# A fused Macaron block in three passes: where the mask and addition of finished tiles, the gate part's copies and a few single steps stand in the hand-written order

## The chip, the cores and the metric

The kernel runs on one core of one Trainium2 chip. TensorE (PE in the profile) does the matmuls, VectorE (DVE) and ScalarE (ACT) read its results and do the elementwise work, GpSimd (POOL) does elementwise work on data in SBUF, and SyncE (SP) issues most transfers. PE writes its products into PSUM banks; a product can start in a bank only when the engines that read the bank's former content are done. Everything is fp32. The metric is the device time in microseconds of one execution, as the median of several runs.

## The reference

The input is 4 x 1024 tokens with an embedding of 1024. The block adds half a clustered feed-forward, then attention, then the same feed-forward again, each on a layer norm of the running sum:

```python
x = x + 0.5 * ffn(layernorm(x))
x = x + attn(layernorm(x))
x = x + 0.5 * ffn(layernorm(x))

def ffn(x):                        # x: 4096 tokens x 1024
    dots = softmax(x @ centroids.T / 0.1)          # 64 clusters
    hits = dots > 0.01
    query_sel = any(hits, axis=1)                  # per token
    row_sel = any(hits, axis=0)[assignments]       # per output, over ALL tokens
    dense = x @ weight.T + bias
    return where(query_sel[:, None] & row_sel[None, :], dense, 0)

def attn(x):                       # 32 query heads, 8 shared key/value heads, D = 32
    q, k, v = x @ Wq + bq, x @ Wk + bk, x @ Wv + bv
    scores = einsum('bsdh,bseh->bsde', q, k) / sqrt(D)   # attention over D, within one token
    return einsum('bsde,bseh->bsdh', softmax(scores), v)
```

The row mask of the feed-forward needs the gates of all tokens. No tile can be finished before all gates are known.

## The kernel before

**Tiles and passes.** The tokens are cut into NT = 32 tiles of 128. Because of the row mask the kernel goes over the tiles three times. The first pass computes the gates and the dense output of the first feed-forward and stores the latter (`d1`) in HBM. The second pass (loop `for s in range(NT + 5)`, L898 to L1016) loads x and `d1`, masks and adds (`first_added`), normalizes, projects to q, k and v, does the attention, adds it (`second_added`), normalizes again and computes the gate part of the second feed-forward. The third pass (L1019 to L1093) computes the rest of the second feed-forward, masks it, adds it and writes the output. Tiles 26 to 31 are "kept" in SBUF from the second pass to the third; the others travel through HBM (`y2`, `xTd`, `d2`).

**Winograd products.** Large products are done for two tiles at once with seven half-size products in place of eight. In the feed-forward this is `winograd` (L258), a generator that yields after each product. Its order is: product 1 into a bank u, product 5 into v, product 2 into p, product 6 accumulated onto u, product 7 into y, product 3 into a further bank, product 4 accumulated onto y. After each product but the second, DVE adds what is ready into the rows of the output d (L270): one addition after products 1, 2, 7, 3 and 4, three after product 6. A product that accumulates onto u has to wait until the earlier addition has read u. Each product is four matmuls of 128x384 (L279); four PSUM banks serve them. The sums of the two tiles' halves that the products 5, 6, 7 and 3 take as input are `token_sums` (L252 to L255, four POOL instructions per pair), and the differences of weight blocks are `weight_sums` (L240). In the second pass `project_two` does the same for q, k and v of tiles 4 to 29 (`PAIRED`), in steps that are set between other PE work; its additions are L733 to L753.

**The gate part.** The columns of the feed-forward weight are cut into three parts; the first two go through the Winograd pairs and the third, with the 64 centroids behind it, is an ordinary product (`ffn_part`, L209). In the second pass `gate_2` issues it: ACT copies the dense part out of the bank (L221), DVE takes the maximum and difference of the gate's logits (L330, L332). `transposed` (L202, L203) turns a normalized tile with eight PE transposes into two banks, each copied out by ACT. `moments` (L159 to L162) computes the layer norm's statistics: bn_stats and bn_aggr on DVE, then a square root on ACT; `normed` (L168 to L177) makes the scales on DVE and normalizes on ACT. `first_added` is a mask on DVE (L388) and an addition on POOL (L399).

**The order is written by hand.** Each engine works through its instructions in the order in which the Python code emits them, and there is no scheduler. So a line that is moved in the code moves each instruction that it issues on that instruction's own engine, past the instructions of the lines it is moved over. Generators (`steps`, `two`, `held`, `normal`, `qsums`) let pieces of several computations be put between each other. The banks and the row buffers (26 of 512 KB, tag "row") are given out in turn.

**Third pass.** For each pair, the loads of the pair two ahead are issued on SP, then POOL makes the sums for the next pair (`ahead_3`), then the seven steps of `winograd` run. `added` (L1038 to L1041) finishes a tile: mask on DVE (L388), addition on DVE (L1040), and the output transfer on ACT's queue. The two `added` of a pair stand behind its last step, and the kept tiles' `added` stand behind the third and the sixth step of the first pairs.

**Drain and start of the second pass.** `held` are two Winograd pairs of the first pass, of which some steps are left to fill the first three rounds of the second. At the end of the second pass (s = NT + 2 and NT + 3) the first Winograd pair of the third pass, tiles 28 and 29, begins.

## Time and profile before

| | |
|---|---|
| median of 3 runs | 1350.83 us (1348.01 to 1351.83) |
| profiled execution | 1344.48 us |
| span of its trace | 1342.8 us, mean granted TensorE clock 0.998 |
| PE busy | 1313.6 us, 98% |
| DVE, POOL, ACT busy | 874.0, 581.8, 524.7 us |
| third pass, pairs | 19.14 us from one to the next (tiles 6 to 23) |
| second pass, two tiles | 34.95 to 36.28 us |

In a line of the timeline the first number is the start and the second the duration, both in us; then come engine, line of the kernel, operation and the tiles written and read. "x8" is the number of instructions put together in the line, and the brackets give the idle time ahead of it and what ended it. A PE line with x8 is four matmuls, each recorded as two. In the list of groups the numbers after the bar are the busy time in us and the mean of one in ns. A line of the windows begins with the window and gives for PE, PEld, DVE, ACT and POOL the busy us with the number of instructions, then the granted clock as a share of full speed, the share of the DMA engines that was busy, and GB/s.

### The profile page before, as it was taken

What the parts mean: (1) busy time and instruction counts of PE and PEld (TensorE: products, weight loads), DVE (VectorE), ACT (ScalarE), POOL (GpSimd) and SP (SyncE); (2) the same over time, 40 slices, a digit from 0 to 9 for tenths busy, and PEclk for the clock granted to TensorE, in tenths of its full rate; (3) what the DMA queues carried; (4) which work ended last, traced back from release to release, by engine and by line L of the source; (5) the groups of instructions that cost most, each with busy time, mean ns of one, the idle gap of its engine ahead of it and who ended that gap; (6) DMA issues with size and microseconds to landing.
All of it is one profiled execution on the core that took longest, in us unless ns stands there. A gap on an engine that the chain in (4) does not pass through costs nothing.

```text
span 1342.8 us, 22211 instructions
## 1 busy us (share of the span) xinstructions
PE 1313.6 (98%) x8486; PEld 823.7 (61%) x8486; DVE 874.0 (65%) x1709; ACT 524.7 (39%) x843; POOL 581.8 (43%) x443
## 2 busy tenths in 40 slices
PE   8999999999999999999999999999999999999998
PEld 7666666666665665666666666666666555555554
DVE  4565544554435368888888888878877358656655
ACT  4443434343411355666666666666633100000000
POOL 3511132232212255666666666666433316544540
PEclk9999999999999999999999999999999999999999
DMA  8477666668514255455656666665641257456421
GB/s 291 89 166 137 162 146 145 160 134 190 115 66 188 74 174 174 145 171 183 190 184 195 189 193 194 197 182 166 195 121 38 73 173 276 154 196 202 162 103 66
DMA packets 295770, 213.42 MB, mean 159 GB/s; under 512 B 240048, under 2 KB 254640, under 8 KB 295664
## 3 DMA queue, kind: packets, MB, share of 16 engines
q1 hardware_dynamic: 277712, 164.00, 44.9%
q0 software_dynamic: 8736, 30.68, 6.2%
q10 hardware_dynamic: 9216, 17.33, 3.4%
q8 instruction: 67, 1.10, 0.4%
q14 instruction: 39, 0.32, 0.1%
HBM read 127.77 MB, written 84.18 MB: 158 GB/s over the span
## 4 chain that ended last, share of the span: by engine, by line
PE 39%; DVE 8%; DMA 4%; issue 4%; POOL 2%; SPq 1%; ACT 1%; DVEq 0%; POOLq 0%; ACTq 0%
PE st L279 15%; PE qs L717 11%; PE ff L209 8%; DVE d L388 3%; DMA qkvd<-qkv 2%; PE tp L202 2%; DVE bn L159 2%; POOL x L864 2%; PE pq L209 2%; PE sc L793 1%; PE po L835 1%; DMA ot<-od 1%; DVE o L847 1%; SPq L767 1%; DMA qk<-qkvd 1%
## 5 line engine op out<-in xcount | busy, mean ns | idle before, releaser
L209 PE MATMUL ff<-wc,xT 128*128 128x320 f32 (+1 forms) x1088 | 307.6, 436 | 1.6 <-ACT wc L492 0.7
L209 PEld LDWEIGHTS ff<-wc,xT 128*128 128x128 f32 x1088 | 204.8, 190 | 92.5 <-ACT xT L203 1.0
L252 POOL TENSOR_TENSOR ts<-xT 128x512 f32<-128x512 f32 x31 | 42.4, 1367 | 296.0 <-PE st L279 187.9
L279 PE MATMUL st<-wc,xT 128*128 128x384 f32 x496 | 170.1, 486 | 0.0
L270 DVE TENSOR_TENSOR d<-st,d 128x384 f32<-128x384 f32 x157 | 86.4, 552 | 123.3 <-PE st L279 121.0
L773 POOL TENSOR_TENSOR kd<-qk,tmask 128x1024 f32<-128x1024 f32 x32 | 60.6, 1894 | 173.3 <-DMA qk<-qkvd 166.2
L279 PE MATMUL st<-wqkv,ts 128*128 128x384 f32 x360 | 123.7, 493 | 11.0 <-DVE d L270 11.0
L279 PEld LDWEIGHTS st<-wc,xT 128*128 128x128 f32 x496 | 94.0, 190 | 63.4 <-issue 0.2
L279 PE MATMUL st<-ws,ts 128*128 128x384 f32 x384 | 131.5, 486 | 0.0
L159 DVE BATCH_NORM_STATS2 bn<-x 128x6 f32<-128x512 f32 x132 | 84.5, 682 | 45.6 <-DMA x<-in_L_attn_x_dram 24.0
L388 DVE SCALAR_TENSOR_TENSOR d<-d,qsel,mask 128x1024 f32<-128x1024 f32 (+2 forms) x68 | 112.9, 1661 | 0.4 <-issue 0.2
L279 PEld LDWEIGHTS st<-wqkv,ts 128*128 128x128 f32 x360 | 68.2, 192 | 63.3 <-issue 19.6
L399 POOL TENSOR_TENSOR x<-x,d 128x1024 f32<-128x1024 f32 x32 | 75.4, 2357 | 71.2 <-DVE d L388 54.8
L717 PE MATMUL qs<-wc,ts_2q 128*128 128x384 f32 x312 | 106.2, 490 | 0.0
L279 PEld LDWEIGHTS st<-ws,ts 128*128 128x128 f32 x384 | 72.7, 190 | 49.4 <-issue 0.8
L162 ACT ACT_TABLE_LOAD x31 | 39.8, 1283 | 147.7 <-DVE mv L161 146.3
L270 DVE TENSOR_TENSOR d<-st,brow 128x384 f32<-128x384 f32 x93 | 51.2, 550 | 66.1 <-PE st L279 66.1
L203 ACT COPY xT<-tp 128x512 f32<-128x512 f32 x138 | 73.1, 581 | 32.6 <-PE tp L202 31.7
L279 PE MATMUL st<-wc,ts 128*128 128x384 f32 x248 | 85.2, 486 | 0.0
L202 PE MATMUL tp<-ident,xn 128*128 128x128 f32 x552 | 75.2, 276 | 8.5 <-ACT xT L203 6.5
L717 PEld LDWEIGHTS qs<-wc,ts_2q 128*128 128x128 f32 x312 | 58.2, 190 | 40.5 <-issue 2.6
L202 PEld LDWEIGHTS tp<-ident,xn 128*128 128x128 f32 x552 | 62.6, 141 | 28.4 <-ACT xT L203 9.3
(122 smaller groups left out, 2081.6 us busy)
## 6 DMA issues: line engine op xcount, KB each, us to landing
x<-in_L_attn_x_dram SPq DMA_DIRECT2D x64, 512.0 KB, 4.4
d<-d SPq DMA_DIRECT2D x64, 512.0 KB, 4.4
out_dram<-x ACTq DMA_DIRECT2D x30, 512.0 KB, 5.1
xb<-in_L_attn_x_dram SPq DMA_DIRECT2D x108, 128.0 KB, 4.6
y<-x POOLq DMA_DIRECT2D x26, 512.0 KB, 3.1
xTd<-xT POOLq DMA_DIRECT2D x26, 512.0 KB, 4.9
xT<-xTd SPq DMA_DIRECT2D x26, 512.0 KB, 4.8
x<-y SPq DMA_DIRECT2D x26, 512.0 KB, 4.8
```

Of the source, the lines that this page charges most:

```text
L159: nc.vector.bn_stats(st[:, i, :], src[:, i * 512 : (i + 1) * 512])
L162: nc.scalar.activation(mv[:, 1:2], mv[:, 1:2], AF.Sqrt, bias=eps)
L202: nc.tensor.transpose(tp[:, j, :], xn[:, k * P : (k + 1) * P], ident)
L203: nc.scalar.copy(t_[:, 4 * h : 4 * h + 4, :], tp)
L209: nc.tensor.matmul(p, src[:, k, :], wts[:, k, lo:hi], start=(k == 0), stop=(k == KT - 1))
L252: nc.gpsimd.tensor_tensor(s1, a21, a22, ALU.add)
L270: nc.vector.tensor_tensor(out, ps, other, ALU.add)
L279: nc.tensor.matmul(ps, src[:, k, :], wts[:, k, :], start=(k == 0 and onto is None), stop=(k == 3), skip_group_check=onto is not None,)
L388: nc.vector.scalar_tensor_tensor(d[:, sl], d[:, sl], qsel[which][:, t : t + 1], mask[:, sl], ALU.mult, ALU.mult)
L399: nc.gpsimd.tensor_tensor(xt[t], xt[t], dt_.pop(t), ALU.add)
L717: nc.tensor.matmul(ps, src[:, k, :], wts[:, k, :], start=(k == 0 and onto is None), stop=(k == 3), skip_group_check=onto is not None,)
L773: nc.gpsimd.tensor_tensor(kd, qk[:, :, D:].unsqueeze(2).to_broadcast([P, NBLK, 4, D]), tmask.unsqueeze(1).unsqueeze(3).to_broadcast([P, NB ...
```

## The change

Four places of the order are changed. The computation stays the same.

In the third pass the mask and addition of a finished pair's tiles stand no longer together behind the pair's last step. They are put off (`done`): one behind the first step and the other behind the third step of the next pair. The kept tiles' come behind the fifth and sixth step.

In the second pass, on odd steps, the gate part of one tile and the transposes of the other are emitted ahead of the statistics of a third. On PE nothing changes places. On ACT the copies L221 and twice L203 go ahead of the square root L162, and on DVE L330 and L332 go ahead of L159 and L161. On step 29, whose successor is not in `PAIRED`, the transposes are emitted by a later line, behind the normalization.

At the start of the second pass the left-over Winograd steps run as two, one and one in the first three rounds in place of one, one and two; two stores on SP go ahead of two loads. The third difference of weights is made a round earlier, and the fourth on POOL in place of DVE.

In the drain, the first three steps of the pair 28, 29 are emitted ahead of the statistics of tile 31.

```diff
-        qsums = weight_sums(wqkv, qts, [nc.gpsimd] * 3 + [nc.vector])
+        qsums = weight_sums(wqkv, qts, [nc.gpsimd] * 4)
...
-            if s == 4:
+            if 3 <= s <= 4:
                 next(qsums)
...
+            if paired and odd and s + 1 in PAIRED:
+                gate_2(a)
+                xT[f] = transposed(xn3.pop(f), f"3_{f}")
             if paired and (not odd or s + 1 not in PAIRED):
                 fo = attend(st, qkv.pop(b)[1], b)
-            if s == 4:
-                next(qsums)
+            if s == NT + 2:
+                dt_[a] = row(f"d3_{a}")
+                steps = winograd(s - 6, s - 5, ss, ts, None, 3)
+                for _ in range(3):
+                    next(steps)
             if has(g):
                 mv = moments(xt[g], f"3_{g}")
...
             if paired:
-                if odd:
-                    if s + 1 in PAIRED:
-                        gate_2(a)
-                    xT[f] = transposed(xn3.pop(f), f"3_{f}")
-                else:
+                if not odd:
                     next(two)
                 between()
...
-                    i = s - 6
-                    if k == 2:
-                        dt_[a] = row(f"d3_{a}")
-                        steps = winograd(i, i + 1, ss, ts, None, 3)
-                    for _ in range(6 - k):
+                    for _ in range(1 if k == 2 else 3):
                         next(steps)
...
-                for _ in range(1 + s // 3):
-                    next(held[s // 3])
-                i = {2: NT - 4, 3: NT - 2}.get(s)
+                for _ in range(2 if s == 1 else 1):
+                    next(held[s // 2])
+                i = {1: NT - 4, 3: NT - 2}.get(s)
                 for i in (i, i + 1) if i else ():
                     nc.sync.dma_start(out=d1[i], in_=dt_.pop(i))
...
+        done = iter(())
         for a in range(0, FIRST_KEPT, 2):
...
             for i in range(7):
                 next(steps)
-                if i in (2, 5):
-                    for t in kept:
-                        added(t)
-                        break
+                for t in done if i in (0, 2) else kept if i in (4, 5) else ():
+                    added(t)
+                    break
...
-            if not last:
-                added(a)
-                added(a + 1)
+            done = iter((a, a + 1))
```

## Prediction

> **What bounds the kernel now.** I read the page's busy times first, then what TensorE (PE) waited for, then the timelines around each of those waits. The page says that one engine fills the span:

> ```profile
> PE 1313.6 (98%) x8486; PEld 823.7 (61%) x8486; DVE 874.0 (65%) x1709; ACT 524.7 (39%) x843; POOL 581.8 (43%) x443
> ```

> The change adds and removes no matmul, so it can only win or lose the remaining 1342.8 - 1313.6 = 29.2 us in which PE stood idle, plus what a low clock adds. The waits of PE, as line waited for, us in total, times, longest:

> ```profile
> PE st L279 <- DVE d L270: 11.0, 10, 2.4
> PE tp L202 <- ACT xT L203: 6.5, 10, 1.1
> ...
> PE qs L717 <- DVE qkv L750: 0.8, 1, 0.8
> ...
> PE qs L717 <- DVE sc L190: 0.5, 1, 0.5
> PE ff L209 <- DVE d L270: 0.4, 1, 0.4
> ```

> Three stalls, then: Winograd products waiting for VectorE (DVE), transposes waiting for copies on ScalarE (ACT), and a few single ones. Everything off PE is hidden unless it feeds one of these.

> **Third pass.** PE and DVE around one pair of tiles:

> ```profile
> 1148.51 2.74 PE L279 MATMUL st<-wc,xT 128*128 128x384 f32 x8
> ...
> 1157.26 5.40 PE L279 MATMUL st<-wqkv,ts 128*128 128x384 f32 x16 [0.84 <-DVE d L270]
> ...
> 1167.65 2.74 PE L279 MATMUL st<-wc,xT 128*128 128x384 f32 x8
> ```

> ```profile
> 1148.71 0.56 DVE L270 TENSOR_TENSOR d<-st,d 128x384 f32<-128x384 f32 x1 [2.02 <-PE st L279]
> 1149.19 1.92 DVE L388 SCALAR_TENSOR_TENSOR d<-d,qsel,mask 128x1024 f32<-128x1024 f32 x1
> 1151.14 2.17 DVE L1040 TENSOR_TENSOR x<-x,d 128x1024 f32<-128x1024 f32 x1
> 1153.24 1.75 DVE L388 SCALAR_TENSOR_TENSOR d<-d,qsel,mask 128x1024 f32<-128x1024 f32 x1
> 1155.02 1.63 DVE L1040 TENSOR_TENSOR x<-x,d 128x1024 f32<-128x1024 f32 x1
> 1156.57 0.54 DVE L270 TENSOR_TENSOR d<-st,brow 128x384 f32<-128x384 f32 x1
> ```

> Products start 2.58 us apart (1148.51, 1151.09, 1153.67), so seven cost 18.06; the pair takes 1167.65 - 1148.51 = 19.14, 1.08 more. The fourth product accumulates onto the first one's bank (`onto=u`), so it must wait for the DVE addition that reads u. That addition is ready at 1151.25 and runs at 1156.57, behind the two `added` calls (7.4 us of L388 and L1040). Nine pairs (6 to 22) start 19.14 apart; pair 4, with two kept tiles' additions in its predecessor, takes 20.17. Lost: 9 x 1.08 + 2.11 = 11.8.

> After: let T count from the pair's first product. The u addition runs at 2.7 to 3.3. `added(a)` follows at 3.3 to 7.4 with the slow pair of durations above (4.1; without GpSimd (POOL) beside it L388 and L1040 take 1.27 and 1.22 at 1086 us, so 2.5). The third product's addition comes at 7.9 to 8.45, `added(a+1)` to 12.5 at worst, the three additions of the fourth product then end at 14.1, that of the fifth at 14.7. The last product, which accumulates onto the fifth's bank, starts at 15.48. Cover: 0.8 us with every L388 and L1040 slow, about 3 otherwise. I take the whole 11.8. The output transfers move with the additions, 3 to 6 us later on ACT's queue, which has no other work in this pass; SyncE's loads into the freed rows (1172.48 to 1181.39 here) then move too, and POOL's token sums with them. The token sums that start at 1165.32 feed a product that starts at 1167.65 + 19.14 + 2.58 = 1189.4; they last 6 us, so 6 us of lateness fits in a lead of 24.

> **Second pass, odd steps.** ACT runs the square root of `moments` ahead of the gate part's copies (L221, L203), and the square root waits for statistics:

> ```profile
> 890.50 0.29 ACT L162 ACTIVATE mv<-mv,eps 128x1 f32<-128x1 f32 x1 [2.04 <-DVE mv L161]
> 890.70 0.35 ACT L221 COPY d<-ff 128x256 f32<-128x256 f32 x1
> 890.95 1.07 ACT L203 COPY xT<-tp 128x512 f32<-128x512 f32 x2
> ```

> ```profile
> 891.59 0.65 PE L202 MATMUL tp<-ident,xn 128*128 128x128 f32 x4 [1.00 <-ACT xT L203]
> ```

> ff ended at 888.1 and ACT was free at 888.45, so the three copies run at 888.45 to 890.1 after the change and the transpose at 891.59 finds its bank. From one odd step's ff to the next the eleven full periods are 34.95 to 36.28 us; the shortest, 34.95, I take as the floor. The sum over it is 6.66, and 1.3 for the first step makes 8.0 (the recorded waits alone, 5.7). PE's own order stays. On DVE the gate's maximum and difference (L330, L332, 0.5 us) now precede bn_stats (1.29 + 0.21). Here they finish before x arrives from POOL at 888.93. In steps where x arrives first, bn and the mask behind it slip by up to 1.8 us (DVE's idle before this bn, 1.76) plus 1.5. What that delays is the mask, POOL's addition behind it and the next projection's additions (L739), which had 0.77 to 1.3 us to spare ahead of their PE reader. I take 6.5, with ends at 0 and 8. The square root itself, later by up to 1.4 us, is needed a step later.

> Step 29 loses: its transpose is not among the early ones and now stands behind square root, scales and the 1.25 us normalization of tile 26. The copies of tile 25 move from 962.81 to about 964.9, and the transpose and the product at 964.02 wait for them: -1.9, once.

> **Start of the second pass.** The fourth weight difference (L240) leaves DVE for POOL, the third moves one step up, the held products of the first pass move up and two stores of d pass two loads on SyncE. The 1.75 us of L240 on DVE at 518.35 stand ahead of bn_stats, the normalization, and the copies and additions that PE awaited at 524.15 (0.87) and 525.60 (0.79). The wait of 0.46 at 515.38 came from a mask on DVE that took 4.23 us at 509.94 while POOL ran L240 (3.44 us from 509.64); with POOL's row pushed 4.6 us on, that pair meets no more. Together 2.1, and the chain's remainder makes 2.3. [...] I take +2.3, ends -2 and +2.7.

> **Drain.**

> ```profile
> 1044.53 4.41 PE L279 MATMUL st<-wqkv,ts 128*128 128x384 f32 x8 [2.38 <-DVE d L270]
> ```

> ```profile
> 1041.61 1.29 DVE L159 BATCH_NORM_STATS2 bn<-x 128x6 f32<-128x512 f32 x2 [4.60 <-POOL x L864]
> ```

> ```profile
> 1044.00:1046.00 2.00, 1.47 (x3) 0.89 (x4) 0.94 (x2) 1.24 (x1) 0.00 (x0) 0.58 0.79 281
> ```

> The two additions PE needs queue behind statistics of tile 31, which wait for x (1041.61). After the change they run first, inside the 4.60 us idle. Saved: 2.38 of wait, 0.37 of the following ff wait. The product also took 4.41, where 2.74 is usual, at a granted clock of 0.58. [...] The row shows the drop directly behind this gap and nowhere else in the drain; the 1.88 us gap at 1136 brought none. I follow the row: ff starts at 1046.15, not 1050.18, gain 4.0, low end 2.4. Statistics of tile 31 slip by 0.5, covered until its transpose at 1062.

> **Sum.** 11.8 + 6.5 - 1.9 + 2.3 + 4.0 = 22.7, against the profiled execution's 1344.48: 1321.8. The median of three runs is 1350.83, 6.4 above that execution; the same share gives 1350.83 x (1 - 22.7/1344.48) = 1328.0.

> **Rivals.**
> - *The stall in the third pass only moves.* POOL's sums and L1035 now meet both separated `added`; if each takes 4.1 us and the u addition starts late, the last or sixth product waits and half of 11.8 stays: 1334. For: the alternating rows above. Against: the cover of 0.8 even then.
> - *The second pass gives nothing.* The later mask takes at L739 what the copies gave: 1328.0 + 6.5 = 1334.5. For: the small spare of 0.77. Against: in the step shown x arrives last.
> - *Slower.* The same mechanism outright: bn behind the gate slips by 1.8 + 1.5 = 3.3 in each of 12 pairs, less 1.3 spare, 2.0 x 12 = 24 lost and 6.5 not gained: 1358.5. It decides from (22.7 - 6.5)/12 = 1.35 us per pair. Against: DVE's idle of 1.76 before bn in the step shown ends on x, not on the gate.

> **How the numbers follow.** The forecast has 0.62, the first rival 0.13, the second 0.13, mixtures near no change 0.05, slower 0.07. A measurement of this kernel can tell about 0.3% (4 us) from no change. Faster 0.62 + 0.13 + 0.13 = 0.88, same 0.05, slower 0.07. Low end: 2 us of the pass-2 and start bounds and 4 of the runs' spread below 1328, 1321; high end: both rivals together, 1328 + 5.9 + 6.5 = 1340, plus 1: 1341. The forecast alone: 1323 to 1333.

> **What would show it.** Right: pairs 4 to 22 start 18.06 apart with no wait on L270; no PE wait on L203 from 530 to 930; the clock stays at 1.00 at 1044; one L203 wait near 964. Wrong: PE waits on L739 at the projection's fifth product, on POOL at 506, or on a DMA in the third pass.

## The result, and the profile after

The changed kernel takes 1326.70 us (median of 6 runs, 1325.35 to 1330.37) against 1349.96 us for the kernel before (6 runs, 1345.33 to 1352.20), a ratio of 0.9836 with a 95% interval of 0.9814 to 0.9859: 22 us, between 19 and 25. The profiled execution has a span of 1323.6 us in place of 1342.8. The waits of PE in it, in the columns of before:

```profile
PE tp L202 <- ACT xn L177: 2.2, 1, 2.2
PE tp L202 <- ACT xT L203: 1.9, 1, 1.9
...
PE sc L793 <- DMA qkvd<-qkv: 0.4, 1, 0.4
PE st L279 <- DVE d L270: 0.3, 1, 0.3
```

The 11.0 us behind L270 have become 0.3 (and those are in the first pass), and the ten waits on L203 are one. Two waits grew by some 0.4 us or are new: 2.2 us on L177 at the very start (1.8 before), in code that the change doesn't touch, and 0.4 us at the attention scores.

**Third pass.** PE around one pair, then DVE in the same stretch (L1038 is the addition of `added`, L1040 before):

```profile
1138.02 2.74 PE L279 MATMUL st<-wc,xT 128*128 128x384 f32 x8
...
1145.76 5.32 PE L279 MATMUL st<-wqkv,ts 128*128 128x384 f32 x16
...
1156.08 2.10 PE L279 MATMUL st<-wc,xT 128*128 128x384 f32 x6
```

```profile
1140.80 0.56 DVE L270 TENSOR_TENSOR d<-st,brow 128x384 f32<-128x384 f32 x1 [2.02 <-PE st L279]
1141.28 1.37 DVE L388 SCALAR_TENSOR_TENSOR d<-d,qsel,mask 128x1024 f32<-128x1024 f32 x1
1142.68 1.63 DVE L1038 TENSOR_TENSOR x<-x,d 128x1024 f32<-128x1024 f32 x1
1145.96 0.56 DVE L270 TENSOR_TENSOR d<-st,d 128x384 f32<-128x384 f32 x1 [1.65 <-PE st L279]
1146.43 1.28 DVE L388 SCALAR_TENSOR_TENSOR d<-d,qsel,mask 128x1024 f32<-128x1024 f32 x1
1147.74 1.22 DVE L1038 TENSOR_TENSOR x<-x,d 128x1024 f32<-128x1024 f32 x1
```

The pair takes 1156.08 - 1138.02 = 18.06 us, and the products run on without brackets. DVE adds u at 1140.80, as soon as it is there. The two `added` need 3.0 and 2.5 us where they took 4.1 and 3.4 before. In these rows they no longer run beside POOL's token sums; in pair 22 of the kernel before, where POOL was idle, each took 2.5 us as well, so the sums are the likely reason.

**Second pass.** ACT in an odd step:

```profile
882.57 0.35 ACT L221 COPY d<-ff 128x256 f32<-128x256 f32 x1
882.82 1.07 ACT L203 COPY xT<-tp 128x512 f32<-128x512 f32 x2
884.97 0.29 ACT L162 ACTIVATE mv<-mv,eps 128x1 f32<-128x1 f32 x1 [1.07 <-DVE mv L161]
```

The copies no longer wait for the square root. Every two tiles take 34.95 us, the floor, from 528.15 to 912.65.

**Step 29.** PE in the kernel before, then PE's one wait on L203 after the change, and the windows from there on:

```profile
963.09 1.09 PE L202 MATMUL tp<-ident,xn 128*128 128x128 f32 x8
964.02 10.49 PE L209 MATMUL pq<-wqkv,xT 128*128 128x384 f32 x32
```

```profile
957.73 1.11 PE L202 MATMUL tp<-ident,xn 128*128 128x128 f32 x4 [1.92 <-ACT xT L203]
958.64 11.75 PE L209 MATMUL pq<-wqkv,xT 128*128 128x384 f32 x32
```

```profile
958.00:960.00 2.00, 2.00 (x7) 1.38 (x7) 1.49 (x3) 1.97 (x5) 0.00 (x0) 0.50 0.98 292
960.00:962.00 2.00, 2.00 (x6) 1.12 (x5) 1.93 (x6) 0.66 (x3) 0.22 (x1) 0.70 0.81 148
```

A wait of 1.92 us, and behind it half the clock for some three microseconds: the projection took 11.75 us, 10.49 before.

**Drain.** PE at the first products of tiles 28 and 29:

```profile
1037.84 2.74 PE L279 MATMUL st<-wqkv,ts 128*128 128x384 f32 x8
1040.42 1.04 PE L202 MATMUL tp<-ident,xn 128*128 128x128 f32 x8
1041.92 1.34 PE L209 MATMUL ff<-wc,xT 128*128 128x320 f32 x4 [0.46 <-DVE d L270]
```

The fourth product takes 2.74 us, without a wait.

The two profiled executions can be set side by side stretch by stretch, each between the starts of the same PE instruction:

| stretch | before | after | difference | forecast |
|---|---|---|---|---|
| start to first full projection (same code in both) | 442.49 | 444.47 | +1.98 | 0 |
| to the first gate product (start of second pass) | 85.79 | 83.68 | -2.11 | -2.3 |
| to the gate product of step 29 | 429.40 | 421.60 | -7.80 | -6.5 |
| to the next gate product (step 29's loss) | 18.69 | 22.50 | +3.81 | +1.9 |
| to the first product of tiles 28, 29 | 57.88 | 57.85 | -0.03 | 0 |
| to the gate product behind the fourth product (drain) | 15.93 | 11.82 | -4.11 | -4.0 |
| to the first product of tile 4 | 78.16 | 78.04 | -0.12 | |
| to the first product of tile 24 (third pass) | 191.37 | 180.60 | -10.77 | -11.8 |
| to the end | 23.09 | 23.04 | -0.05 | 0 |
| sum | 1342.8 | 1323.6 | -19.2 | -22.7 |

This is one execution of each. The second row can come out smaller with the same code, as the second pass's block alone shows below.

### The profile page after: what moved, and what is told of

Read it like the earlier page. It is cut to its first block, busy times and chain, and to the rows that moved or that the text cites. A ratio compares the mean times of both kernels' runs of the same rounds, so it can differ in the third digit from the quotient of the medians.

```text
span 1323.6 us, 22208 instructions
## 1 busy us (share of the span) xinstructions
PE 1310.4 (99%) x8486; PEld 826.0 (62%) x8486; DVE 858.6 (65%) x1708; ACT 524.9 (40%) x843; POOL 575.4 (43%) x444
## 4 chain that ended last, share of the span: by engine, by line
PE 91%; DVE 4%; DMA 2%; ACT 2%; issue 1%; ACTq 0%; DVEq 0%; SPq 0%
PE st L279 39%; PE ff L209 21%; PE qs L717 17%; PE tp L202 4%; PE pq L209 4%; PE sc L793 2%; PE po L835 2%; DMA x<-in_L_attn_x_dram 1%; DVE bn L159 1%; DMA scd<-sc 1%; DVE d L270 0%; PE tpw L487 0%; ACT xT L203 0%; DVE d L388 0%; PE pm L382 0%
## 5 line engine op out<-in xcount | busy, mean ns | idle before, releaser
L209 PE MATMUL ff<-wc,xT 128*128 128x320 f32 (+1 forms) x1088 | 307.5, 436 | 1.5 <-ACT xT L203 0.6
L209 PEld LDWEIGHTS ff<-wc,xT 128*128 128x128 f32 x1088 | 204.7, 190 | 92.4 <-issue 1.0
L279 PE MATMUL st<-wc,xT 128*128 128x384 f32 x496 | 170.2, 486 | 0.0
L270 DVE TENSOR_TENSOR d<-st,d 128x384 f32<-128x384 f32 x157 | 86.0, 550 | 122.3 <-PE st L279 121.1
L279 PEld LDWEIGHTS st<-wc,xT 128*128 128x128 f32 x496 | 94.0, 190 | 63.6 <-issue 0.4
L279 PE MATMUL st<-ws,ts 128*128 128x384 f32 x384 | 131.6, 487 | 0.3 <-DVE d L270 0.3
L279 PE MATMUL st<-wqkv,ts 128*128 128x384 f32 x360 | 121.3, 486 | 0.0
L388 DVE SCALAR_TENSOR_TENSOR d<-d,qsel,mask 128x1024 f32<-128x1024 f32 (+2 forms) x68 | 106.3, 1563 | 0.1
L717 PE MATMUL qs<-wc,ts_2q 128*128 128x384 f32 x312 | 106.2, 490 | 0.0
L159 DVE BATCH_NORM_STATS2 bn<-x 128x6 f32<-128x512 f32 x132 | 84.3, 680 | 31.2 <-DMA x<-in_L_attn_x_dram 28.5
L279 PEld LDWEIGHTS st<-ws,ts 128*128 128x128 f32 x384 | 72.6, 190 | 50.2 <-issue 2.1
L279 PEld LDWEIGHTS st<-wqkv,ts 128*128 128x128 f32 x360 | 68.3, 190 | 48.1 <-issue 0.8
L203 ACT COPY xT<-tp 128x512 f32<-128x512 f32 x138 | 73.2, 581 | 30.4 <-PE tp L202 29.5
L279 PE MATMUL st<-wc,ts 128*128 128x384 f32 x248 | 85.1, 486 | 0.0
L270 DVE TENSOR_TENSOR d<-st,brow 128x384 f32<-128x384 f32 x93 | 51.2, 550 | 52.1 <-PE st L279 52.0
L717 PEld LDWEIGHTS qs<-wc,ts_2q 128*128 128x128 f32 x312 | 58.2, 190 | 40.5 <-issue 2.6
L202 PE MATMUL tp<-ident,xn 128*128 128x128 f32 x552 | 74.3, 278 | 4.2 <-ACT xn L177 2.2
L864 POOL TENSOR_TENSOR x<-x,ot 128x1024 f32<-128x1024 f32 x32 | 77.1, 2408 | 2.5
```

Source lines behind the costliest of these rows:

```text
L159: nc.vector.bn_stats(st[:, i, :], src[:, i * 512 : (i + 1) * 512])
L202: nc.tensor.transpose(tp[:, j, :], xn[:, k * P : (k + 1) * P], ident)
L203: nc.scalar.copy(t_[:, 4 * h : 4 * h + 4, :], tp)
L209: nc.tensor.matmul(p, src[:, k, :], wts[:, k, lo:hi], start=(k == 0), stop=(k == KT - 1))
L270: nc.vector.tensor_tensor(out, ps, other, ALU.add)
L279: nc.tensor.matmul(ps, src[:, k, :], wts[:, k, :], start=(k == 0 and onto is None), stop=(k == 3), skip_group_check=onto is not None,)
```

## The experiments

**Each part alone.** The four parts of the change were put singly into the kernel before: the third pass's loop, the second pass's block, the start (differences of weights and held products), and the drain. Six of the runs below were executed once each: the start alone, the drain alone, the differences undone, both additions together, the statistics first and the gaps. The 22 executions of the kernel before beside the first two of these spread from 1341.3 to 1350.7 us, so what is said of these six is read from their traces and not from their times. The third pass alone:

```diff
+        done = iter(())
         for a in range(0, FIRST_KEPT, 2):
...
-                if i in (2, 5):
-                    for t in kept:
-                        added(t)
-                        break
+                for t in done if i in (0, 2) else kept if i in (4, 5) else ():
+                    added(t)
+                    break
...
-            if not last:
-                added(a)
-                added(a + 1)
+            done = iter((a, a + 1))
```

> The kernel before with the third pass's edit alone. Theory: every pair from 4 on starts 18.06 us after the one ahead, with no wait on L270; from tile 4's first product to tile 24's first product 180.6 us in place of 191.4, so about 10.8 us off the time of before, ratio 0.992. Rival (the stall only moves to another product): 185 to 186 us and a new wait on L270 at the sixth or seventh product. The gap of 2.4 us in the drain is still there; if every gap of that length brings a low clock, its product takes 4.4 us again, and if it depends on where the gap falls, it may take 2.74.

Measured: a ratio of 0.9929 to the kernel before (0.9901 to 0.9957). From tile 4's to tile 24's first product 180.59 us, in a pair:

```profile
1131.55 2.74 PE L279 MATMUL st<-wc,xT 128*128 128x384 f32 x8
...
1139.29 5.32 PE L279 MATMUL st<-wqkv,ts 128*128 128x384 f32 x16
...
1149.61 0.81 PE L279 MATMUL st<-wc,xT 128*128 128x384 f32 x2
```

1149.61 - 1131.55 = 18.06, with no bracket on the fourth product. The third pass's part gives its 10.8 us by itself, and the stall did not move to another product. The gap in the drain was 2.71 us here, and its product took 2.82: no low clock (granted 1.00 from 1049 to 1053 us) behind a longer gap than that of before.

The second pass's block alone:

```diff
+            if paired and odd and s + 1 in PAIRED:
+                gate_2(a)
+                xT[f] = transposed(xn3.pop(f), f"3_{f}")
             if paired and (not odd or s + 1 not in PAIRED):
                 fo = attend(st, qkv.pop(b)[1], b)
...
-                if odd:
-                    if s + 1 in PAIRED:
-                        gate_2(a)
-                    xT[f] = transposed(xn3.pop(f), f"3_{f}")
-                else:
+                if not odd:
                     next(two)
```

> The kernel before with the second pass's edit alone (gate part and transposes ahead of the statistics, step 29 as in the change). Theory: two tiles take 34.95 us in all steps between the first and the last gate product, 7 us less in sum than before, and step 29 loses 1.9 us, or up to 3.8 if its gap brings a low clock; together 3 to 5 us off, ratio 0.996 to 0.998. Rival (DVE's later statistics and masks take it back): a wait on L739 at the projection and no gain.

Measured: ratio 0.9963 (0.9951 to 0.9975). No wait on L203 between the first step and step 29, where it was 1.95 us; this time the clock stayed at 1.00 behind it. From the first gate product to the projection of tile 30 it took 429.95 us in place of 435.74, 5.8 less. The projection did not wait on L739 anywhere.

The stretch ahead of it, from the first full projection to the first gate product, took 84.37 us in place of 85.79, though up to that product this run's order is that of the kernel before: the block acts first in the step of this gate product. The waits of 0.46 and 0.87 were not there, because a mask happened to start ahead of POOL's weight difference; the run with the differences undone comes back to it.

The start alone:

```diff
-        qsums = weight_sums(wqkv, qts, [nc.gpsimd] * 3 + [nc.vector])
+        qsums = weight_sums(wqkv, qts, [nc.gpsimd] * 4)
...
-            if s == 4:
+            if 3 <= s <= 4:
                 next(qsums)
...
-            if s == 4:
-                next(qsums)
...
-                for _ in range(1 + s // 3):
-                    next(held[s // 3])
-                i = {2: NT - 4, 3: NT - 2}.get(s)
+                for _ in range(2 if s == 1 else 1):
+                    next(held[s // 2])
+                i = {1: NT - 4, 3: NT - 2}.get(s)
```

> The kernel before with the edit at the start of the second pass alone (held products a round earlier, weight differences all on POOL and one a round earlier). Theory: from the first full projection's start to the first gate product 83.7 us in place of 85.8, the waits of 0.46, 0.87 and 0.79 gone, nothing else changed. [...]

Measured: 84.09 us, 1.7 less than before and 0.4 short of the theory. Of the four profiles with the order of before in this stretch, three have 85.71 to 87.56 (the last with a low clock) and one 84.37, so the gain differs from one execution to the next. The waits of 0.46, 0.87 and 0.79 are gone, but a new one of 0.79 stands at the attention scores:

```profile
504.94 1.06 PE L793 MATMUL sc<-kd,qk 32*32 32x128 f32 x64 [0.79 <-DMA qkvd<-qkv]
```

The line names a transfer, the store of the next tile's q, k and v, which is no input of these scores; POOL had made their keys a step earlier (490.82 in the profile of the change). But the scores are written where the last attention product lay (both are tiles of the one buffer "att"), and DVE still reads that in L847. DVE in this run shows why it is late:

```profile
498.93 3.02 DVE L388 SCALAR_TENSOR_TENSOR d<-d,qsel,mask 128x1024 f32<-128x1024 f32 x1
...
503.17 1.52 DVE L847 SCALAR_TENSOR_TENSOR o<-po,tmask,o 128x256 f32<-128x256 f32 x3
```

The mask takes 3.02 us where 1.27 is usual, beside POOL's third difference (L240, here 3.46 us from 497.40). Eight profiles have the difference at this place. In them the mask took 2.60 to 3.27 us and PE waited 0.37 to 1.05, in each 2.22 or 2.23 less than the mask took; in three profiles without it the mask took 1.27 or 1.28 and PE did not wait. So the wait is the mask's. And in all eight the mask ended 1.09 to 1.10 us behind the end of POOL's L240. In this run 1.93 us of L240 were left when the mask came, and the mask took 1.75 us longer than the usual 1.27: it lost about what was left of that instruction, and not its whole length of 3.46.

The drain alone:

```diff
+            if s == NT + 2:
+                dt_[a] = row(f"d3_{a}")
+                steps = winograd(s - 6, s - 5, ss, ts, None, 3)
+                for _ in range(3):
+                    next(steps)
             if has(g):
                 mv = moments(xt[g], f"3_{g}")
...
-                    i = s - 6
-                    if k == 2:
-                        dt_[a] = row(f"d3_{a}")
-                        steps = winograd(i, i + 1, ss, ts, None, 3)
-                    for _ in range(6 - k):
+                    for _ in range(1 if k == 2 else 3):
                         next(steps)
```

> The kernel before with the edit in the drain alone. Theory: the wait of 2.4 us on L270 in the drain is gone and the fourth product takes 2.74 us, so from the first product of tiles 28 and 29 to the gate product behind the transposes 11.8 us in place of 15.9. Rival (the low clock comes from elsewhere): the product takes 4.4 us still, 13.5 us.

Measured: 11.81 us, and no wait at the fourth product. The low clock went with the gap, as the theory had it: the product takes 2.74 us, 4.41 before. This profile has a low clock at another place, though, behind two short waits of 0.88 and 0.79 us at the start of the second pass; the kernel before has nearly the same two waits (0.87 and 0.79) and full speed behind them, a granted clock of 1.00 and 2.85 us for the product that takes 4.54 here:

```profile
528.39 4.54 PE L717 MATMUL qs<-wc,xT 128*128 128x384 f32 x8 [0.79 <-DVE qkv L750]
```

**The start with the differences undone.** In the changed kernel:

```diff
-        qsums = weight_sums(wqkv, qts, [nc.gpsimd] * 4)
+        qsums = weight_sums(wqkv, qts, [nc.gpsimd] * 3 + [nc.vector])
...
-            if 3 <= s <= 4:
+            if s == 4:
                 next(qsums)
...
+            if s == 4:
+                next(qsums)
             if s == NT + 2:
```

> The changed kernel with the third and fourth weight difference where they were before (third on POOL and fourth on DVE, both in round 4). Theory: the 1.75 us on DVE bring back the waits of 0.87 and 0.79 and the collision the one of 0.46, and from the first full projection to the first gate product it takes 85.3 to 85.8 us in place of 83.7. Rival (the held products' places did it): 83.7 to 84.

Measured: 85.22 us. The waits of 0.82 and 0.78 are back; the one of 0.46 is not, and that at the scores is gone. So the places of the differences are worth 0.9 to 1.5 us here (the eight profiles with the change's places have 83.68 to 84.35); of the 1.60 that the two waits cost, the wait at the scores takes the rest back, wholly or in part. The 0.46 is another matter. DVE's mask and POOL's L240 around it, in the kernel before and then in the second pass's block alone, whose order in this stretch is the same:

```profile
509.94 4.23 DVE L388 SCALAR_TENSOR_TENSOR d<-d,qsel,mask 128x1024 f32<-128x1024 f32 x1
509.64 3.44 POOL L240 TENSOR_TENSOR wc<-wqkv 128x1536 f32<-128x1536 f32 x1
```

```profile
513.10 1.19 DVE L388 SCALAR_TENSOR_TENSOR d<-d,qsel,mask 128x1024 f32<-128x1024 f32 x1
513.69 3.90 POOL L240 TENSOR_TENSOR wc<-wqkv 128x1536 f32<-128x1536 f32 x1
```

Before, L240 came 0.30 us ahead of the mask and the mask took 4.23 us; in the second run it came 0.59 us behind, and the mask took 1.19. PE's wait of 0.46 was gone, and that of 0.87 with it, as DVE came to the work behind the mask earlier. With the differences undone L240 starts two microseconds behind the mask (513.62 and 511.44; the mask takes 2.33), and there is no wait of 0.46 either. So the 0.46 hangs on which of the two starts first, by some tenths of a microsecond, and with the order of before it can fall either way. What the held products' places add to that is not shown.

**Step 29 mended.** The transposes ahead of that step's statistics:

```diff
+            if paired and odd and s + 1 not in PAIRED:
+                xT[f] = transposed(xn3.pop(f), f"3_{f}")
             if has(g):
                 mv = moments(xt[g], f"3_{g}")
```

Beside it ran the changed kernel once more, and the same with eight transposes of the identity, whose result nothing reads, in the idle time at the start:

```diff
         columns(7)
+        for i in range(8):
+            nc.tensor.transpose(bank(f"fill{i}")[:, :P], ident, ident)
         xT[0] = transposed(xn.pop(0), "1_0")
```

> The changed kernel once more, on the chip of the next three. Every theory: a ratio of 0.984 to the kernel before, within 0.003. The waits of 1.9 us at step 29 and of about 2 us at the start are there again; whether a low clock follows them may differ from the first profile.

> The changed kernel with the transposes of step 29 emitted ahead of that step's statistics. Theory: the wait of 1.9 us on L203 there is gone, and with it the low clock that followed in the first profile; from the gate product of step 29 to the projection of tile 30 6.3 us in place of 8.9, in all 2 to 4 us below the changed kernel, ratio 0.981 to 0.983. Rival (the banks are held by something else, DVE's gate or the attention): the wait stays at over 1 us.

> The last one with eight more transposes of the identity in PE's idle time ahead of the first token tile's transposes. Theory: these fill most of the 2.2 us gap there, so that the transposes behind it always take 1.1 and not 2.0 us; 0 to 1.5 us below the last one. Rival: PE runs them at half speed past the point at which the normalized tile is there, and loses about 0.3 us.

Measured, on one chip against the same runs of the kernel before: the changed kernel 0.9852 (0.9826 to 0.9877), 1324.94 us; with step 29 mended 0.9842 (0.9821 to 0.9864), 1323.67 us; with the eight transposes too 0.9820 (0.9799 to 0.9841), 1320.67 us. The second ratio is above the 0.981 to 0.983 expected, though its interval reaches down to them, and the last kernel is 3.0 us below the one ahead of it, more than the 1.5 expected. The intervals of the three overlap, though each of the four executions of the last (1320.50 to 1321.55) is quicker than each of the five ahead of it (1322.43 to 1324.83). What happened where is in the traces. ACT and PE at step 29, mended:

```profile
952.52 1.05 ACT L203 COPY xT<-tp 128x512 f32<-128x512 f32 x2
955.08 0.30 ACT L162 ACTIVATE mv<-mv,eps 128x1 f32<-128x1 f32 x1 [1.50 <-DVE mv L161]
955.90 1.24 ACT L177 ACTIVATE xn<-x,sc 128x1024 f32<-128x1024 f32 x1 [0.53 <-DVE sc L170]
```

```profile
955.17 1.09 PE L202 MATMUL tp<-ident,xn 128*128 128x128 f32 x8
956.10 4.36 PE L209 MATMUL pq<-wqkv,xT 128*128 128x384 f32 x13
```

The copies run two microseconds ahead of the square root and the transpose has no bracket: 956.10 - 949.77 = 6.33 us from the gate product to the projection, as expected, 8.89 in the change. From the first gate product to the first product of the drain it is 498.78 us against 501.95 for the change, 3.2 less, although the next gate product now waits 0.62 us for DVE. At the start, PE with the eight transposes:

```profile
8.49 0.71 PE L496 MATMUL fill<-ident 128*128 128x128 f32 x4 [1.10 <-DVE wc L490]
9.08 1.06 PE L202 MATMUL tp<-ident,xn 128*128 128x128 f32 x8
```

The largest gap there is 1.10 us in place of 2.25, and the token transposes take 1.06 us, 1.97 in the profile of the change. They are not late. This is one profile; that they will always do so isn't shown.

**Both additions together, behind the first step.**

```diff
-                for t in done if i in (0, 2) else kept if i in (4, 5) else ():
+                for t in done if i == 0 else ():
+                    added(t)
+                for t in kept if i in (4, 5) else ():
                     added(t)
                     break
```

> The changed kernel with both additions of the finished pair behind the first step of the next pair, not one there and one behind the third. Theory: what matters is that the first product's addition comes ahead of them; they end at 10.7 us at worst and the fourth product's additions are ready at 10.48, so pairs still start 18.06 us apart without a wait. Rival (it is the single placing that counts): a wait on L270 of 0.5 us or more at the sixth or seventh product in each pair, 18.6 us or more.

Measured: 18.06 us a pair and no wait on L270 in the third pass. DVE:

```profile
1143.30 0.56 DVE L270 TENSOR_TENSOR d<-st,brow 128x384 f32<-128x384 f32 x1 [2.02 <-PE st L279]
1143.78 1.28 DVE L388 SCALAR_TENSOR_TENSOR d<-d,qsel,mask 128x1024 f32<-128x1024 f32 x1
1145.09 1.63 DVE L1038 TENSOR_TENSOR x<-x,d 128x1024 f32<-128x1024 f32 x1
1146.64 1.27 DVE L388 SCALAR_TENSOR_TENSOR d<-d,qsel,mask 128x1024 f32<-128x1024 f32 x1
1147.95 1.23 DVE L1038 TENSOR_TENSOR x<-x,d 128x1024 f32<-128x1024 f32 x1
1149.09 0.55 DVE L270 TENSOR_TENSOR d<-st,d 128x384 f32<-128x384 f32 x1
```

That they are put singly is not what gives the gain in this pass. It is enough that u's addition comes first.

**Statistics first on DVE.** In the changed kernel bn_stats and bn_aggr go back ahead of the gate; the square root stays behind the copies:

```diff
             if paired and odd and s + 1 in PAIRED:
+                mv = moments(xt[g], f"3_{g}", False)
                 gate_2(a)
                 xT[f] = transposed(xn3.pop(f), f"3_{f}")
...
-            if has(g):
+            if paired and odd and s + 1 in PAIRED:
+                nc.scalar.activation(mv[:, 1:2], mv[:, 1:2], AF.Sqrt, bias=eps)
+            elif has(g):
                 mv = moments(xt[g], f"3_{g}")
```

(With `False`, `moments` leaves out the square root.)

> The changed kernel with bn_stats and bn_aggr put back ahead of the gate part on DVE; only the square root on ACT stays behind the copies. Theory: what PE waited for was ACT's order, so the second pass keeps its period of 34.95 us per two tiles and shows no wait on L203 before step 29. Rival (the gate's maximum and difference hold the bank): waits of 0.3 to 1 us at the transposes in the steps where x comes late, up to 7 us in sum.

Measured: no wait of the transposes on the copies ahead of step 29 (there 1.78 us), and a single one of 0.66 at a gate product, on the gate's difference (L333 here). So ACT's order is what had to change; DVE's order is worth about 1 us in the whole pass (from the first gate product to that of step 29 422.65 us, against 421.38 to 421.60 in the eight other profiles with the second pass's block; it was 429.40 before).

**Gaps of two sizes.** What happens to the clock when PE idles for two or three microseconds? In the third pass of the changed kernel:

```diff
             for i in range(7):
+                if i == 0:
+                    for t in done:
+                        added(t)
+                    for j in range(1 if a % 4 else 2) if 4 < a < 22 else ():
+                        idle = small.tile([P, 1], F32, tag="gmx", name=f"idle{j}_{a}")
+                        nc.vector.tensor_reduce(idle, mask, AX.X, ALU.max)
                 next(steps)
-                for t in done if i in (0, 2) else kept if i in (4, 5) else ():
+                for t in kept if i in (4, 5) else ():
                     added(t)
                     break
```

(The additions stand ahead of the pair's first step again, and the maxima behind them, which nothing reads, put u's addition off further.)

> The changed kernel with both additions ahead of the first product's addition, as before the change, and behind them on DVE one or two maxima of 1.2 us that nothing reads, in pairs 6 to 20 (one in pairs 6, 10, 14 and 18, two in 8, 12, 16 and 20). PE then idles about 2 and 3.2 us ahead of the fourth product at eight places. If the low clock depends on where a gap falls and not on its length alone, some of the products behind the 2 us gaps take 4.4 us and some 2.74, and those behind 3.2 us more often 4.4; a pair with the low clock costs about 1.8 us more. [...]

Measured, PE at gaps of both sizes:

```profile
1154.41 5.40 PE L279 MATMUL st<-wqkv,ts 128*128 128x384 f32 x16 [1.97 <-DVE d L270]
1175.80 5.40 PE L279 MATMUL st<-wqkv,ts 128*128 128x384 f32 x16 [3.09 <-DVE d L270]
...
1217.47 7.09 PE L279 MATMUL st<-wqkv,ts 128*128 128x384 f32 x16 [3.10 <-DVE d L270]
...
1260.83 5.40 PE L279 MATMUL st<-wqkv,ts 128*128 128x384 f32 x16 [3.10 <-DVE d L270]
...
1302.49 7.09 PE L279 MATMUL st<-wqkv,ts 128*128 128x384 f32 x16 [3.10 <-DVE d L270]
```

Four equal gaps of 3.1 us: two are followed by a product pair of 7.09 us, with a granted clock of 0.50 in 1219.47 to 1221.47 and 1304.49 to 1306.49, and two by 5.40 at 1.00. So at this length the gap alone does not settle the clock. The low clock expected behind some of the four of 1.97 did not come. A low clock costs 1.7 us here.

## Why the prediction was right, point by point

The forecast was 1328.0 us with a range of 1321 to 1341; the median is 1326.7. The span fell by 19.2 us and the sum named 22.7. Each term can be read from the table. The mechanisms named for the large terms are the ones that the runs show. That the sum came within 1.3 us of the median owes something to luck: 1.0 too much in the third pass and 1.3 too little in the second cancel, and step 29 and the start of the program went the other way by 3.9 in the profile.

- *Third pass, 11.8: the mechanism is right, the size is 1.0 too large.* The step that failed is "Nine pairs (6 to 22) start 19.14 apart", and the table of the profile before has it too ("tiles 6 to 23"). The ninth stall, that of tile 22, does not exist: from 1301.65 to 1319.71 it is 18.06, where POOL has no more sums to make and DVE is through in time. 8 x 1.08 + 2.11 = 10.75, and 10.77 was measured. The list of waits would have told: ten waits in all, one of them the drain's and one pair 4's, leave eight. The rival in which the stall only moves is excluded by the third pass alone and by the run with both additions together.
- *Second pass, 6.5: right, 1.3 too small.* The 1.5 us that I held back for DVE were not needed; nothing waited on L739, and the rival that ends slower did not begin to show. The floor, 34.95 in each step, was reached: 7.8 of the 8.0 named as the upper end.
- *Step 29, -1.9: the wait is right to the tenth (1.92), the price is not.* It was 3.81 in the profile, the other half of it from the low clock behind the wait. The step that failed is that the wait was costed at its length alone, while in the drain I had let the clock follow a gap of 2.38. What was allowed for one gap of some two microseconds had to be allowed for the other, as a chance: behind the same wait the second pass alone (1.95) kept the full clock.
- *Start, 2.3: 2.11, with its terms shifted.* The three waits went in these two profiles. Two of them were also missing in one of four profiles with the order of before, so the gain is 2.11 against this execution and would be 0.7 at most against that one (84.37 us, against 83.68 to 84.35 with the change's order). PE did not wait on POOL at 506. The slow mask beside a weight difference on POOL came at another place, 2.60 to 3.27 us where 1.27 is usual, and made PE wait at the scores, by way of a bank, for 0.37 to 1.05 us. For the low end of -2 that the prediction gives this term no run shows a source: the start alone gained 1.7 us with a wait of 0.79 at the scores in it.
- *Drain, 4.0: 4.11.* I took the row, with the low clock (0.58) directly behind the gap of 2.38 us, and the drain alone shows it right: the low clock went with the gap, and the product takes 2.74 us. Yet in the run of the third pass alone a gap of 2.71 us at the same place had none (granted 1.00), and there removing it would have been worth 14.67 - 11.82 = 2.9. The value taken was right for the profile, not for every run.
- *The unchanged start, 0: +1.98.* In this profile PE idled 2.25 us ahead of the first tile's transposes and ran them at half clock (granted 0.50 from 9.11 to 11.11; 1.97 us for 1.09), which made 1.4 of it. That part of the program is the same in both. It is one reason why the spans differ by only 19.2 and the medians by 23.3. The other is that the profiled execution of before, 1344.48, was quicker than each of the six timed runs of its kernel (1345.33 and more), while that of the change, 1325.35, is as quick as the quickest of its own. What made the slower executions of before slower is not shown; no trace of them was kept.
- *The range.* Its low end is named as 2 and 4 us below 1328.0, which is 1322 and not 1321. Nothing hangs on it.

## What to carry to other kernels

When an accumulating product must wait for a reader of its bank, ask what stands ahead of that reader on its engine, and move only that: here one addition of 0.55 us had to come ahead of 7.4 us of work that nobody awaited, and how the rest was spread made no difference (18.06 us a pair either way). A reordering is only as good as the rare steps that take another path through the code: one step of the second pass gave 3.8 us back in the profile, and could be seen in the order of the instructions beforehand. A wait of some two microseconds on TensorE, or two shorter ones close together, is to be costed with and without the clock that may follow it: of 22 waits of 1.91 to 3.10 us here 12 had a low one behind them, as did one pair of 0.88 and 0.79. And a wait that hangs on which of two engines comes first by some tenths of a microsecond (here 0.30 ahead or 0.59 behind) is to be looked for in more than one profile.

## What the runs showed of the hardware that was not expected

In these runs the clock behind a gap is not decided by the gap's length alone. Behind the first 100 us of the thirteen profiles of this case PE waited 33 times for 1.3 to 3.1 us. Of 11 gaps under 1.9 us none was followed by a granted clock under 0.9. Of 22 from 1.91 to 3.10 us 12 were: gaps of 1.92, 1.98 and 2.07 among them, while one of 2.71 and two of 3.1 were not. The same wait at step 29 of the second pass, 1.92 to 2.17 us long in five profiles, dropped the clock in four, and left it at 1.00 in the fifth (1.95). Where one product took the drop, it cost 1.7 to 1.8 us.

Where a gap falls can be read from the records of the clock. Each of the 13 low stretches in the middle of the profiles lasts 3.41 us, and in the run with gaps of two sizes they lie on a grid of that step: they begin at 959.01, 1112.61, 1218.42 and 1303.76 us, which is 45, 31 and 25 steps of 3.413 us apart. Two gaps of 3.1 us of that run, each from the step of the grid with most of its idle time to the next step:

```profile
1215.01:1218.42 3.41, 0.95 (x3) 0.68 (x4) 2.87 (x4) 0.00 (x0) 0.00 (x0) 1.00 0.94 310
1218.42:1221.83 3.41, 3.41 (x7) 1.71 (x6) 0.00 (x0) 0.00 (x0) 0.00 (x0) 0.50 0.90 330
```

```profile
1174.05:1177.46 3.41, 1.66 (x5) 1.06 (x6) 2.16 (x4) 0.00 (x0) 0.00 (x0) 1.00 1.03 338
1177.47:1180.88 3.41, 3.41 (x12) 2.07 (x11) 1.58 (x3) 0.00 (x0) 0.00 (x0) 1.00 0.83 263
```

A line of the waits can name a transfer for a wait that DVE caused: the scores' wait follows the duration of a mask some instructions upstream to 0.01 us in eight profiles.
